# Expert rows in half blocks: eight blocks shared by two experts

## The chip, the cores and the metric

The kernel runs on one core of one Trainium2 chip. Times are device microseconds of the whole program. A time given for a kernel is the median of several runs; a profile is one execution, and its span runs from the first to the last instruction. PE multiplies matrices (PEld loads its weights), DVE, ACT and POOL are the vector, scalar and GpSimd engines, and SP issues most transfers. POOL also issues every transfer whose rows are chosen by an index (a gather or a scatter).

## The reference

Two layers act on `x`, 8 x 256 x 512 in single precision. The first is a gated long convolution; only what comes after it is touched by the change. The second is a mixture of experts on 2,048 tokens of 512 numbers:

```python
scores = sigmoid(xf @ gate_w.T)                    # 2048 x 8
topk_w, topk_idx = top_k(scores, 2)
topk_w = topk_w / (topk_w.sum(-1, keepdims=True) + 1e-20) * 2.5
shared_out = silu(xf @ shared_wg.T) * (xf @ shared_wu.T) @ shared_wd.T
h = silu(einsum('td,efd->etf', xf, exp_wg)) * einsum('td,efd->etf', xf, exp_wu)
all_out = einsum('etf,edf->etd', h, exp_wd)        # 8 experts, width 352
out = x + shared_out + sum of topk_w * all_out of the token's two experts
```

`xf` is the layer-normalised result of the first layer. Every token goes to two of the eight experts, so 4,096 rows in all are to be multiplied, and how many fall to each expert is known only when the scores are.

## The kernel before

**Stages.** The convolution runs over 32 heads with PE as its work horse (`conv_products`, L393). While it runs, 16 tiles of 128 tokens are normalised, written to `xn_d` in DRAM, and routed in four chunks. The shared expert's products (`up_step` L678, `down_step` L725) are a list of steps spread over the later heads; the last ones come after the convolution. Then come the experts' blocks.

**The table.** `route_places` (L647) gives every pair of token and expert a place: expert e owns 2,048 places, filled in order. POOL scatters an entry (token number, weight) of eight bytes to each place of a DRAM `table`. After the last chunk, `block_experts` (L778) works out from the eight counts, on DVE, which expert each block of 128 rows has (`ek`) and which column of the table it takes (`pick`, one column per block with a single one in it). `load_table` (L823) brings the table back as `tab`, 128 rows of 128 places. `quarters_of` (L839) spreads its token numbers by quarters of 32 rows, and `slots` (L850) multiplies them with `pick`: the results are, for each block, the DRAM rows to gather (`src`), the rows of the output to add to (`row`) and the weights (`gate`).

**The blocks.** There are at most 39 blocks: `NBLK` at L37. The first 36 (`NSURE`) always run; the last three are in a branch (`rest_of_blocks`, L1201), which every engine reaches ahead of block 18 and takes only if the count says so. A block has, in order:

- `gather` (L1048): four indirect transfers of POOL, each 128 rows of 128 numbers.
- `load_ek` (L1062): PE reads the expert into a register.
- `block_T` (L1069): DVE transposes the rows by 32 x 32 squares into `xT`.
- `block_up` (L1110): eight products of PE, 128 rows by 352 columns, whose weights' address is the register's; ACT's sigmoid and two multiplications on DVE.
- `block_hT` (L1153): sixteen small transposes on DVE.
- `block_down` (L1168): three products of PE, 128 rows by 512 columns; ACT scales the result by `gate`; POOL scatters the 128 rows into `out`, adding to what is there.

The trace shows a single-precision product as two records. What order the work has is written out by hand in the last loop (L1212): in round k, rows are gathered for block k + 4 and transposed for block k + 2, block k is multiplied up, and block k - 2 down. Each engine runs its instructions in the order written. Buffers: four for the gathered rows, three for `xT`, `h`, `hT` and `y`, and two banks pairs for PE's results. All scatters write the same tensor `out`, at rows that the program text doesn't know.

**Around the change.** The last steps of the shared expert stand between the table and the first block: three steps, then `slots`, one step, the first gathers, and four down steps with `block_T` of the first three blocks between them (L1036 to L1090). Constants come from POOL at the start (`iota`, L176).

Of the kernel before, what the change touches and what calls it, by code (L numbers as in the profile page):

```python
# [36 lines left out]
NBLK = 2 * NTOK // P + NEXP - 1  # L37
CPE = NTOK // P

NSURE = NBLK - 3  # L40
Q = 32
NQ = P // Q

# [22 lines left out]
def tile_xattn_moe(  # L66
# [123 lines left out]
    blockno = iota("blockno", NBLK, 1, 0)  # L190
    thresh = iota("thresh", CPE, P, 0)
    quarter = const.tile([P, 1], F32, name="quarter")
    for q in range(NQ):
        G.memset(quarter[q * Q : (q + 1) * Q], float(q))
# [582 lines left out]

    def block_experts():  # L778
        def g(name, s, dtype=F32):
            return const.tile(s, dtype, name=name)  # L780

        V.tensor_tensor(place, place, base, ALU.subtract)
        full = g("full", [P, NEXP, CPE])
# [9 lines left out]
        ends = g("ends", [P, NEXP])  # L793
        V.tensor_copy(ends[:, 0:1], nblk[:, 0:1])
        for e in range(1, NEXP):
            V.tensor_tensor(ends[:, e : e + 1], ends[:, e - 1 : e], nblk[:, e : e + 1], ALU.add)
        gap = g("gap", [P, NEXP])
        V.tensor_scalar(gap, nblk, -1.0, float(CPE), ALU.mult, ALU.add)
        full_k = [P, NBLK, NEXP - 1]
        past = g("past", full_k)  # L800
# [3 lines left out]
            ends[:, : NEXP - 1].unsqueeze(1).to_broadcast(full_k),  # L804
            ALU.is_ge,
        )
        ek = g("ek", [P, NBLK], I32)
        with nc.allow_low_precision(reason="whole numbers below 8"):
            V.tensor_reduce(ek, past, AX.X, ALU.add)
        V.tensor_tensor(  # L810
            past, past, gap[:, : NEXP - 1].unsqueeze(1).to_broadcast(full_k), ALU.mult
        )
        col = g("col", [P, NBLK])
        V.tensor_reduce(col, past, AX.X, ALU.add)
        V.tensor_tensor(col, col, blockno, ALU.add)
        pick = g("pick", [P, NBLK])
        V.tensor_scalar(pick, col, lane, None, ALU.is_equal)

        used = g("used", [P, 1], I32)
        V.tensor_copy(used, ends[:, NEXP - 1 :])  # L820
        return ek, pick, used

    def load_table():  # L823

        tab = const.tile([P, P, 2], F32, name="tab")
        ins = S.dma_start(
            out=tab.rearrange("p b f -> p (b f)"),
            in_=table.rearrange("(p b) f -> p (b f)", b=P),
        )
        for s in scatters:  # L830
            tc.add_manual_dep(
                ins.ins,
                s.ins.name,
                mybir.DependencyInfo(mybir.DependencyClass.Sync, mybir.DependencyReason.DATA),
                reason="the table's rows come from all of them",
            )
        return tab

    def quarters_of(tab):  # L839
        by_quarter = const.tile([P, NQ, NQ, Q], F32, name="by_quarter")  # L840
        V.tensor_copy(
            by_quarter,
            tab[:, :, 0]
            .rearrange("p (c b) -> p c b", b=Q)
            .unsqueeze(2)
            .to_broadcast([P, NQ, NQ, Q]),
        )
        return by_quarter

    def slots(tab, by_quarter, pick):  # L850
        def g(name, s, dtype=F32):
            return const.tile(s, dtype, name=name)


        ps = ps_tp.tile([P, 2 + NQ, NBLK], F32, tag="tp", name="slots_ps")
        for f in range(2):
            T.matmul(ps[:, f, :], lhsT=tab[:, :, f], rhs=pick, start=True, stop=True)
        for c in range(NQ):
            T.matmul(
                ps[:, 2 + c, :],  # L860
                lhsT=by_quarter[:, c].rearrange("p q b -> p (q b)"),
                rhs=pick,
                start=True,
                stop=True,
            )

        spare = g("spare", [P, NBLK])
        V.tensor_scalar(spare, ps[:, 0, :], 0.0, lane, ALU.is_equal, ALU.mult)
        row = g("row", [P, NBLK], I32)
        V.scalar_tensor_tensor(row, ps[:, 0, :], float(NTOK), spare, ALU.add, ALU.add)  # L870
        gate = g("gate", [P, NBLK])
        V.tensor_copy(gate, ps[:, 1, :])
        src = g("src", [P, NQ, NBLK], I32)
        for c in range(NQ):
            V.tensor_scalar_add(spare, ps[:, 2 + c, :], float(NTOK))
            V.tensor_scalar(src[:, c], spare, float(NQ), quarter, ALU.mult, ALU.add)
        return src, row, gate
# [24 lines left out]
    skip_products(0)  # L902

# [129 lines left out]
    ek, pick, used = block_experts()  # L1033
    tab = load_table()
    settle()
    for n in range(3):  # L1036
        step()
        if n == 2:
            by_quarter = quarters_of(tab)
        settle()  # L1040
    src, row, gate = slots(tab, by_quarter, pick)
# [6 lines left out]
    def gather(k):  # L1048
        if k >= NBLK:
            return  # L1050
        xgs[k] = (rows if k < NSURE else spare).tile([P, NQ, P], F32, tag="xg", name=f"xg_{k}")
        for c in range(NQ):
            G.indirect_dma_start(  # L1053
                out=xgs[k][:, c, :],
                out_offset=None,
                in_=xn_q,
                in_offset=bass.IndirectOffsetOnAxis(ap=src[:, c, k : k + 1], axis=0),
# [4 lines left out]
    def load_ek(k):  # L1062
        if k < NBLK:
            eks[k] = nc.values_load(
                ek[0:1, k : k + 1], engines=[PE], min_val=0, max_val=min(k, NEXP - 1),
                skip_runtime_bounds_check_because="a block's expert is a count of at most seven",
            )

    def block_T(k):  # L1069

        if k >= NBLK:
            return
        own = (rows, 3) if k < NSURE else (spare, 1)
        xTs[k] = own[0].tile([P, NLB, NQ, Q], F32, tag="xT", name=f"xT_{k}", bufs=own[1])
        V.transpose(
            xTs[k].rearrange("p k c b -> p c k b"),
            xgs.pop(k).rearrange("p c (k a) -> p c k a", a=Q),
# [3 lines left out]
    AHEAD = 2  # L1081
    for k in range(AHEAD + 2):
        gather(k)
    for k in range(AHEAD):
        load_ek(k)
    for k in range(TPC):
        step()
        settle()
        if k <= AHEAD:
            block_T(k)  # L1090
# [19 lines left out]
    def block_up(k, last):  # L1110
        n = min(k + 1, NEXP)
        ps = (ps_b if k < NSURE else ps_spare).tile([P, 2, L], F32, tag="up", name=f"up_{k}")
        wk = wgu_sb[:, :n].rearrange("p e f -> p (e f)")
        for m in range(2):
            for j in range(NLB):
                T.matmul(  # L1116
                    ps[:, m, :FF],
                    lhsT=xTs[k][:, j].rearrange("p c b -> p (c b)"),
                    rhs=wk[:, bass.ds(eks[k] * NGU + (m * NLB + j) * FF, FF)],
                    start=(j == 0),  # L1120
                    stop=(j == NLB - 1),
                )
        hk = (blk if k < NSURE else spare).tile([P, FF], F32, tag="h", name=f"h_{k}")
        A.activation(hk, ps[:, 0, :FF], AF.Sigmoid)  # L1124
        V.tensor_tensor(hk, hk, ps[:, 0, :FF], ALU.mult)  # L1125
        xTs.pop(k)
        if not last:
            V.tensor_tensor(hk, hk, ps[:, 1, :FF], ALU.mult)
# [24 lines left out]
    def block_hT(k):  # L1153
# [3 lines left out]
        for c in range(NQ):  # L1157
# [10 lines left out]
    def block_down(k):  # L1168
        n = min(k + 1, NEXP)
# [4 lines left out]
        wk = wd_sb[:, :n].rearrange("p e f -> p (e f)")  # L1174
        hT = hTb.pop(k)
        for ft, (_, fw) in enumerate(F_TILES):
            T.matmul(  # L1177
                ps,
                lhsT=hT[:fw, ft].rearrange("p c b -> p (c b)"),
                rhs=wk[:fw, bass.ds(eks[k] * NWD + ft * L, L)],  # L1180
                start=(ft == 0),
                stop=(ft == NF - 1),
            )
        y = (blk if k < NSURE else spare).tile([P, L], F32, tag="y", name=f"ys_{k}")
        A.activation(y, ps, AF.Copy, scale=gate[:, k : k + 1])
        G.indirect_dma_start(  # L1186
# [132 lines left out]
```

## Time and profile before

| what | value |
|---|---|
| median of 3 runs | 807.13 us (806.12 to 812.91) |
| profiled execution, own time | 791.86 us |
| its span | 790.1 us |
| PE busy | 768.2 us, 97% |
| DVE, POOL, ACT busy | 535.1, 472.7, 201.8 us |
| experts' up products (L1116) | 176.2 us, 576 records |
| experts' down products (L1177) | 98.6 us, 216 records |
| gathers (L1053) | 144, 1,019 ns each |
| scatters (L1186) | 36, 1,616 ns each |
| first up product, last record of a down product | 511.13, 776.5 us |

A line of the page's groups has the source line, the engine and the operation, what is written and read by the program's names, how many there were, then their busy time, the mean length of one in ns, and the idle time of the engine ahead of them with what ended it. Mean lengths on PE are longer than the distance from one record to the next, since products overlap. A line of a timeline has the start, the length, the engine, the line, the operation and, in brackets, the idle time before. The 68 halves and 36 blocks that the text counts come from the reference's own inputs.

### The profile page before, as it was taken

To read this page: it belongs to the slowest core of one execution; us is meant where nothing else is said; L and a number is where in the kernel's file an instruction comes from. 1 tells how busy PE (TensorE), PEld (TensorE's weight loads), DVE (VectorE), ACT (ScalarE), POOL (GpSimd) and SP (SyncE) were. 2 spreads that over 40 slices of the span, in tenths; PEclk is the share of its full clock that TensorE was granted. 3 is DMA by queue.
4 is the path that set the end of the run, shared out by engine and by line. 5 is a ranking of instruction groups with operands and counts; after the bars stand their busy time and mean duration, and the time that the engine had idled before them with its cause. 6 is when DMAs were issued, how large, how long until landed. Compare 5 with 4: busy or idle time off the path is not lost. (4 is left out here: it accounts for less than half of the span.)

```text
span 790.1 us, 8491 instructions
## 1 busy us (share of the span) xinstructions
PE 768.2 (97%) x2383; PEld 353.7 (45%) x2383; DVE 535.1 (68%) x1209; ACT 201.8 (26%) x382; POOL 472.7 (60%) x474
## 2 busy tenths in 40 slices
PE   8999999999999999999999999999999999999993
PEld 4333334433333443333443444365555555555551
DVE  3678868768567768557765163189778778778760
ACT  2222353443153344134323200011111111111111
POOL 7877784378373469372640043756777757777721
PEclk9999999999999999999999999999999999999997
DMA  7585433324414234312100780396444434344433
GB/s 253 174 298 175 153 114 127 120 35 127 147 46 140 92 50 140 114 47 87 63 12 27 304 347 24 103 263 135 73 68 77 74 56 74 69 75 78 69 45 40
DMA packets 52143, 89.10 MB, mean 113 GB/s; under 512 B 8833, under 2 KB 24065, under 8 KB 50945
## 3 DMA queue, kind: packets, MB, share of 16 engines
q1 hardware_dynamic: 36960, 61.77, 24.4%
q0 software_dynamic: 10816, 18.92, 13.9%
q10 hardware_dynamic: 4320, 7.87, 2.9%
q8 instruction: 21, 0.34, 0.2%
q14 instruction: 26, 0.20, 0.1%
HBM read 66.34 MB, written 22.18 MB: 112 GB/s over the span
## 5 line engine op out<-in xcount | busy, mean ns | idle before, releaser
L416 PE MATMUL cv<-kv,tz 128*64 128x512 f32 (+2 forms) x720 | 190.1, 607 | 0.2 <-POOL kv L376 0.2
L1053 POOL DMA_INDIRECT xg<-xn_d,src x144 | 146.8, 1019 | 62.2 <-issue 46.4
L1116 PE MATMUL up<-wgu_sb,xT 128*128 (+1 forms) x576 | 176.2, 459 | 2.3 <-DVE x L757 1.4
L688 PE MATMUL gu<-xfT,wsh 128*128 128x512 f32 x352 | 156.7, 598 | 1.2 <-issue 1.2
L1160 DVE STREAM_TRANSPOSE hTb<-h 32x96 f32<-32x96 f32 (+1 forms) x560 | 146.3, 261 | 8.2
L376 POOL TENSOR_TENSOR kv<-vT,ctxT 128x512 f32<-128x512 f32 x128 | 133.1, 1072 | 19.0 <-issue 6.2
L1116 PEld LDWEIGHTS up<-wgu_sb,xT 128*128 128x128 f32 x576 | 109.0, 190 | 73.3 <-issue 17.1
L416 PEld LDWEIGHTS cv<-kv,tz 128*64 128x64 f32 (+2 forms) x720 | 60.8, 150 | 119.5 <-issue 97.7
L688 PEld LDWEIGHTS gu<-xfT,wsh 128*128 128x128 f32 x352 | 67.1, 192 | 85.7 <-issue 84.5
L1177 PE MATMUL y<-wd_sb,hTb 128*128 (+3 forms) x216 | 98.6, 592 | 0.8 <-ACT hTb L1149 0.8
L478 DVE TENSOR_TENSOR prod<-cv,ctxT 128x1024 f32<-128x1024 f32 x64 | 78.2, 1221 | 16.4 <-PE cv L416 14.7
L662 POOL DMA_INDIRECT table<-entries,to x32 | 31.8, 993 | 90.5 <-DVE at L658 81.9
L1186 POOL DMA_INDIRECT out_dram<-ys,row x36 | 58.2, 1616 | 41.6 <-issue 24.0
L487 DVE TENSOR_REDUCE convT<-prod 128x128 f32<-128x1024 f32 x64 | 78.1, 1220 | 2.2
L732 PE MATMUL dn<-wshd,hT 128*128 128x512 f32 x160 | 70.2, 593 | 0.0
L1177 PEld LDWEIGHTS y<-wd_sb,hTb 128*128 128x128 f32 (+1 forms) x216 | 41.0, 190 | 43.1 <-issue 34.7
L1124 ACT ACTIVATE h<-up 128x352 f32<-128x352 f32 x36 | 16.7, 463 | 167.0 <-PE up L1116 167.0
L702 ACT ACTIVATE sg<-gu 128x512 f32<-128x512 f32 (+1 forms) x24 | 14.3, 596 | 166.4 <-PE gu L688 166.4
L532 POOL TENSOR_TENSOR skip<-ctxT,w 128x512 f32<-128x512 f32 x16 | 17.2, 1076 | 59.4 <-ACT w L524 30.2
L1125 DVE TENSOR_TENSOR h<-h,up 128x352 f32<-128x352 f32 x36 | 18.6, 517 | 43.6 <-ACT h L1124 43.6
L416 PE MATMUL cv<-kv,td 128*128 128x512 f32 x88 | 47.2, 618 | 0.0
L732 PEld LDWEIGHTS dn<-wshd,hT 128*128 128x128 f32 x160 | 30.2, 190 | 37.6 <-issue 37.6
(149 smaller groups left out, 602.3 us busy)
## 6 DMA issues: line engine op xcount, KB each, us to landing
tz<-in_toep_dram SPq DMA_DIRECT2D x32, 384.0 KB, 3.4
wgu_sb<-in_egu_dram SPq DMA_DIRECT2D x8, 1408.0 KB, 16.3
ctxT<-in_cT_dram SPq DMA_DIRECT2D x16, 384.0 KB, 4.8
x<-in_xv_dram SPq DMA_DIRECT2D x16, 256.0 KB, 3.6
x<-in_x_dram SPq DMA_DIRECT2D x16, 256.0 KB, 4.7
xn_d<-xn ACTq DMA_DIRECT2D x16, 256.0 KB, 2.3
out_dram<-x SPq DMA_DIRECT2D x16, 256.0 KB, 2.4
wd_sb<-in_ed_dram SPq DMA_DIRECT2D x8, 512.0 KB, 11.8
```

The costliest lines, as they stand in the source:

```text
L376: G.tensor_tensor(kv[:, mb], vT[t][:, at, :, cols].unsqueeze(2).to_broadcast([P, B, NH, NH]), ctxT[t][:, at, :, cols].unsqueeze(3).to_broa ...
L416: T.matmul(banks[lb][cols], lhsT=w, rhs=x, start=first, stop=left[lb][here[0]] == 0,)
L478: V.tensor_tensor(prod, ps.rearrange("p k b j i -> p (k b) j i"), ctxT[t][:, 2 + 2 * n : 4 + 2 * n, :, cols] .rearrange("p k b i -> p (k b ...
L487: V.tensor_reduce(convT[t][:, two, :, cols].rearrange("p k b j -> p (k b) j"), prod, AX.X, ALU.add)
L662: ins = G.indirect_dma_start(out=table, out_offset=bass.IndirectOffsetOnAxis(ap=to[:, i : i + 1], axis=0), in_=entry[:, i, n, :], in_offse ...
L688: T.matmul(ps, lhsT=wsh[:, k, m0 : m0 + m], rhs=rhs[k], start=(k == 0), stop=(k == NLB - 1))
L732: T.matmul(ps, lhsT=hTs[c][:, ft, i * P : (i + 1) * P], rhs=wshd[:, ft, :], start=(ft == 0), stop=False,)
L1053: G.indirect_dma_start(out=xgs[k][:, c, :], out_offset=None, in_=xn_q, in_offset=bass.IndirectOffsetOnAxis(ap=src[:, c, k : k + 1], axis=0 ...
L1116: T.matmul(ps[:, m, :FF], lhsT=xTs[k][:, j].rearrange("p c b -> p (c b)"), rhs=wk[:, bass.ds(eks[k] * NGU + (m * NLB + j) * FF, FF)], star ...
L1160: V.transpose(hT[q * Q : (q + 1) * Q, :n, c], hk[c * Q : (c + 1) * Q, q * NF * Q : (q * NF + n) * Q].rearrange("p (t a) -> p t a", a=Q),)
L1177: T.matmul(ps, lhsT=hT[:fw, ft].rearrange("p c b -> p (c b)"), rhs=wk[:fw, bass.ds(eks[k] * NWD + ft * L, L)], start=(ft == 0), stop=(ft = ...
L1186: G.indirect_dma_start(out=out, out_offset=bass.IndirectOffsetOnAxis(ap=row[:, k : k + 1], axis=0), in_=y, in_offset=None, bounds_check=NT ...
```

## The change

Rows are counted in halves of 64. Every expert's first half goes to a fixed place: the second half of one of eight shared blocks (`NMIX`), whose expert there is a constant of the program. What is left of an expert fills whole blocks of its own, of which 26 (`NPURE`) always run; whole blocks beyond the 26 and odd halves are put one after another into the first halves of the eight shared blocks, with their expert in a register, and, when these are full, into 16 half blocks in the branch. So 34 blocks always run in place of 36. The eight shared blocks stand at positions 7, 10, 13 and so on to 28 of the order.

A shared block multiplies each of its two halves with its own expert's weights, by products of 64 columns of the array each, and its result goes out by two scatters of 64 rows, the second of which is issued in the middle of the next round's gathers. The table is read back shifted by 64 places, by three transfers. The arithmetic on the counts has a second part (`half_experts`), and the shared blocks' rows a second set of products (`half_slots`).

The core of the diff:

```diff
+HALVES = 2 * NTOK // P
+NPURE, NMIX, NCOND = 26, NEXP, 16
+NSURE, NHALF = NPURE + NMIX, NMIX + NCOND
+NBLK = NPURE + NHALF
...
-    blockno = iota("blockno", NBLK, 1, 0)
-    thresh = iota("thresh", CPE, P, 0)
-    quarter = const.tile([P, 1], F32, name="quarter")
-    for q in range(NQ):
-        G.memset(quarter[q * Q : (q + 1) * Q], float(q))
...
+    def half_experts(nblk, ends):
+        odd = g("odd", [P, NEXP])
+        V.scalar_tensor_tensor(odd, nblk, -float(P), place, ALU.mult, ALU.add)
+        V.tensor_scalar(odd, odd, float(HP), None, ALU.is_gt)
...
+        for e in range(NEXP):
+            at = NEXP + e
+            V.tensor_tensor(
+                ends[:, at : at + 1],
+                ends[:, at - 1 : at] if e else begin,
+                odd[:, e : e + 1],
+                ALU.add,
+            )
...
+        any_half = g("any_half", [P, 2, NHALF])
+        for n in range(2):
+            V.tensor_scalar(any_half[:, n], half, float(-n), lane2, ALU.add, ALU.is_equal)
+        first_half = g("first_half", [P, NEXP])
+        V.tensor_scalar(first_half, first_block, lane, None, ALU.is_equal)
...
+        return eh, any_half, first_half, used
...
         tab = const.tile([P, P, 2], F32, name="tab")
+        body = (P - 1) * P
+        for to, first, n in (
+            (tab[: P - 1], HP, body),
+            (tab[P - 1 :, :HP], HP + body, HP),
+            (tab[P - 1 :, HP:], 0, HP),
+        ):
+            ins = S.dma_start(
+                out=to.rearrange("p b f -> p (b f)"),
+                in_=table[first : first + n].rearrange("(p b) f -> p (b f)", b=to.shape[1]),
+            )
...
+    def half_slots(any_half, first_half):
+        ps = ps_tp.tile([P, 2, NQ, NHALF], F32, tag="tp", name="halves_ps")
+        for f in range(2):
+            quarter = [by_quarter[f][:, c].rearrange("p q b -> p (q b)") for c in range(NQ)]
+            for c in range(2):
+                for n in range(2):
+                    T.matmul(
+                        ps[:, f, c],
+                        lhsT=quarter[2 * n + c],
+                        rhs=any_half[:, n],
+                        start=(n == 0),
+                        stop=(n == 1),
+                    )
+                T.matmul(
+                    ps[:, f, 2 + c, :NMIX],
+                    lhsT=quarter[2 + c],
+                    rhs=first_half,
+                    start=True,
+                    stop=True,
+                )
+        rows_h = g("rows_h", [P, NHALF])
+        for n, m in enumerate((NHALF, NMIX)):
...
+            for c in range(2):
+                A.copy(rows_h[c * Q : (c + 1) * Q, :m], ps[c * Q : (c + 1) * Q, 0, 2 * n + c, :m])
+                at = slice((2 * n + c) * Q, (2 * n + c + 1) * Q)
+                A.copy(gate[at, cols], ps[at, 1, 2 * n + c, :m])
...
+            lay_rows(row[at, to], rows_h[at, :m], f"spare_{n}", at)
...
     skip_products(0)
+    lane2 = iota("lane2", 1, 0, 2)
+    blockno = iota("blockno", NPURE, 1, 0)
+    halfno = iota("halfno", NHALF, 1, 0, base=2 * NPURE)
+    thresh = iota("thresh", CPE, P, 0, base=P)
+    expert_thresh = iota("expert_thresh", NEXP - 1, HALVES, 0, base=HALVES)
+    first_block = iota("first_block", NEXP, CPE, 0, base=-1)
...
+    def gather(b):
+        xgs[b] = (rows if b < NSURE else spare).tile([P, NQ, P], F32, tag="xg", name=f"xg_{b}")
+        for c in range(rows_in(b) // Q):
+            if c == 3:
+                send_late()
             G.indirect_dma_start(
...
+    FIRST = 7
+    seq = list(range(NPURE))
+    for i in range(NMIX):
+        seq.insert(FIRST + 3 * i, NPURE + i)
...
+        if k == 0:
+            eh, any_half, first_half, used = half_experts(nblk, ends)
+            turn_quarters(1, tab, A.copy)
+        if k == 2:
+            half_slots(any_half, first_half)
...
             for j in range(NLB):
+                for at, e in eks[k]:
+                    T.matmul(
+                        ps[at, m, :FF],
+                        lhsT=xTs[k][:, j].rearrange("p c b -> p (c b)")[:, at],
+                        rhs=weights(wgu_sb, k, e, (m * NLB + j) * FF, FF),
+                        start=(j == 0),
+                        stop=(j == NLB - 1),
+                    )
...
+        def send(at, col):
+            G.indirect_dma_start(
+                out=out,
...
+                in_=y[at],
...
+        send(eks[k][0][0], k)
+        if len(eks[k]) > 1:
+            late.append((send, slice(HP, P), k + NHALF))
...
-        with tc.If(more > NSURE):
-            for k in range(NSURE, NBLK):
+        with tc.If(more > 2 * NPURE + NMIX):
+            for b in range(NSURE, NBLK):
...
-        if k == NSURE // 2:
+        if k == NSURE - 8:
             rest_of_blocks()
```

The down products are written for the two halves in the same way.

## The prediction

> **What bounds the kernel now.** I read the page's busy shares first, then the stages by windows, then the timelines of PE and POOL in the last third, and the DMA view around one load. Two lines of the page (busy time, share, instructions; then a group with its count, busy time and mean) and one row of the windows (busy us of PE, PEld, DVE, ACT, POOL, then clock and DMA share):
>
> ```profile
> PE 768.2 (97%) x2383; PEld 353.7 (45%) x2383; DVE 535.1 (68%) x1209; ACT 201.8 (26%) x382; POOL 472.7 (60%) x474
> ...
> L1186 POOL DMA_INDIRECT out_dram<-ys,row x36 | 58.2, 1616 | 41.6 <-issue 24.0
> ```
> ```profile
> 542.00:630.00 88.00, 88.00 (x266) 50.15 (x265) 71.80 (x231) 13.80 (x24) 69.39 (x62) 1.00 0.43 74
> ```
>
> PE is never idle in the expert stage: it binds there. But POOL's 69 of 88 us hide something. In the next timelines (start, length, engine, line, operation, idle before), PE's down products of two blocks in a row start 7.31 us apart, and POOL's scatters 7.25 us (7.241 over 28 of them, less the branch), with only 0.3 us of handover between its instructions:
>
> ```profile
> 591.24 2.74 PE L1177 MATMUL y<-wd_sb,hTb 128*128 x6
> ...
> 598.55 1.88 PE L1177 MATMUL y<-wd_sb,hTb 128*128 x4
> ```
> ```profile
> 560.78 1.63 POOL L1186 DMA_INDIRECT out_dram<-ys,row  x1 [0.30 <-issue]
> 562.72 1.06 POOL L1053 DMA_INDIRECT xg<-xn_d,src  x1 [0.30 <-issue]
> 564.09 1.01 POOL L1053 DMA_INDIRECT xg<-xn_d,src  x1 [0.31 <-issue]
> 565.40 1.01 POOL L1053 DMA_INDIRECT xg<-xn_d,src  x1 [0.30 <-issue]
> 566.71 1.01 POOL L1053 DMA_INDIRECT xg<-xn_d,src  x1 [0.30 <-issue]
> 568.03 1.63 POOL L1186 DMA_INDIRECT out_dram<-ys,row  x1 [0.30 <-issue]
> ```
>
> So POOL, with four gathers (1.313 us each with handover) and a scatter (1.94 us) a block, has 0.07 us a block to spare. Nor can scatters go closer. At the end, with the gathers gone:
>
> ```profile
> 769.27 1.55 POOL L1186 DMA_INDIRECT out_dram<-ys,row  x1 [3.94 <-issue]
> 774.71 1.55 POOL L1186 DMA_INDIRECT out_dram<-ys,row  x1 [3.88 <-ACT hTb L1149]
> 780.14 1.55 POOL L1186 DMA_INDIRECT out_dram<-ys,row  x1 [3.89 <-issue]
> ```
>
> They follow each other every 5.44 us: 1.55 us of issue, then 3.89 us until the transfer has landed (4.7 us from its start by the tile's view) and the next may start. All write `out` at rows known only at run time, so each waits for the last. With 780.14 the end of the kernel hangs on this chain, not on PE, done at 776.5.
>
> Ahead of the experts, PE stands at the table's load:
>
> ```profile
> 483.52 0.64 PE L857 MATMUL slots_ps<-pick,tab 128*128 128x39 f32 x4 [1.10 <-DMA tab<-table]
> 483.99 1.06 PE L859 MATMUL slots_ps<-pick,by_quarter 128*128 128x39 f32 x8
> 484.88 5.38 PE L688 MATMUL gu<-xfT,wsh 128*128 128x512 f32 x8
> ```
>
> **What the skill says.** *DMA: Bandwidth & Descriptors*, "Why a DMA increments its semaphore by 16 and not by 1": a transfer issued by SP runs on the largest number of engines up to 16 that divides its slowest dimension, so 128 partitions take 16 and 127 take one. The DMA view of 481 to 484 us agrees for 128:
>
> ```profile
> DMA  0000000000000000013323687740000000000000
> ...
> q1 hardware_dynamic: 144, 0.13, 12.6%
> ```
>
> The load's 128 rows and 16 small packets take 12.6% of 16 engines times 3 us, 6.05 us in all, some 46 ns a row, within 11 slices of 0.075 us; no run shows 127. The price of a row alone, 42 to 43 ns for 1 KiB, is in *Advanced Engine Details and Errata*, "Clock Domains". *TensorEngine Tiling*, "Key Properties": half-width tiles run independently, changing the tiling mode drains the array. The trace agrees:
>
> ```profile
> 96.99 1.02 PE L416 MATMUL cv<-kv,td 128*128 128x512 f32 x2
> 97.94 2.96 PE L416 MATMUL cv<-kv,tz 128*64 128x512 f32 x16
> 100.83 1.12 PE L416 MATMUL cv<-kv,td 128*128 128x512 f32 x2
> ```
>
> The 16 records (eight 128x64, eight 64x64) start to next start take 2.89 us where the same work at full use (0.429 us a full record, as in the down products: 8/2 + 8/4 of them) takes 2.57. By the groups split by form, 128x64 records cost 244 ns of busy time against 461 for full ones: they run in pairs. *Perfetto Trace Analysis*, "DMA Instruction — SWDGE (GPSIMD)": the recorded time of such a transfer is the writing of its descriptors, not the movement. So 1.62 us of a scatter should fall with its rows.
>
> **The change, part by part.** Routing the reference's inputs gives 554, 506, 572, 453, 532, 450, 523 and 506 rows per expert: 36 blocks of 128, or 68 halves of 64. Eight are fixed; 28 whole blocks and 4 odd halves leave exactly 60, so the branch (over 60) isn't taken, as before (36 of 36).
>
> *Two blocks fewer.* PE loses 2 x 7.31 = 14.6 us; POOL's steps are counted below.
>
> *Eight shared blocks on PE.* Each of their 22 half-width products pairs with its neighbour, so a block costs one block. Mode changes: about 0.15 us in and 0.19 out in the stretch above; both an up and a down stretch, 0.68 us a block, 5.4 us in all. Bounds: 0, and 58 us if nothing pairs; PE gains 9.2 us net. Register arithmetic stays at one instruction for each register-addressed product, hidden in the queue today (PE waits 0.9 us on it in all).
>
> *POOL's chain.* A shared block keeps four gathers and has two scatters of 64 rows, the second put between the third and fourth gather of the next round. Each waits for the landing before it. Not in this trace: a scatter of 64 rows. Its issue lies between 0.81 (half) and 1.62 us; I take 0.9, near half. The wait behind it lies between 2.3 (landing halved) and 3.89; I take 3.1. First to second: 0.9 + 0.31 + 3 x 1.313 = 5.15 us (the landing is covered). Second to the next block's: 0.9 + 3.1 = 4.0, since one gather covers only 2.5. Together 9.15, 1.91 more than 7.24. Behind that wait stand the next gathers. From block 1's scatter to block 29's, before, took 207.8 us, with 5.13 for the branch; to the last, 33.2 more: 241.1. After: 26 steps of 7.24 (188.2), 7 x 1.91 (13.4), the branch 5.1, then, gathers gone, 5.44 + 4.0 + 4.0 + 4 x 5.44 = 35.2: **241.9**. PE over the same rounds, 26 x 7.31 + 7 x 0.68 + 0.9 at the branch, is 196: POOL comes 11 us behind, under the two rounds that gathers run ahead, so PE isn't starved, but the end is POOL's: +0.8 us instead of -9.2. The bounds give -7 and +20.
>
> *The table's load* becomes three: 127 rows on one engine, 127 x 42 ns = 5.3 us and two short ones behind, instead of 0.8: **+4.6 us**, all of it PE's idle time, since `slots` stands next in its queue and DVE's copy waits too. Bound below: +0.7 us, two more issues of 0.33, if it is spread.
>
> *half_slots* adds 12 products, 24 records at 0.113 us ((484.88 - 483.52)/12): **+2.7 us** on PE, between down steps that have no gap.
>
> *Clock.* At 484.88 eight records took 5.2 us against 3.5: the half clock after the idle stretch cost 1.7 us. *A longer idle time* costs between nothing and as much again; +0.5.
>
> *At nothing:* half_experts, some 29 DVE instructions of 0.2 to 0.5 us, 7 us, in DVE's idle 493.8 to 500; if it ran over, the x additions slip, with 3 us to spare before half_slots. Its ACT copies lie in ACT's idle 25 us; `lay_rows` ends before the down step (5.5 us) does. The iotas moved past skip_products (about 1.2 us of POOL) fit its 4.39 us wait for vT. `slots` on DVE is 1 us shorter, before gathers that POOL does well ahead. The branch, larger inside, is skipped as before; it moves from block 18 to round 26, past eight rounds of each queue, and costs POOL the same wait for its last landing (640.45 to 647.52 between two of its transfers) and PE 0.9 us; both are counted above.
>
> Sum: 0.8 + 4.6 + 2.7 + 0.5 = +8.6 us on 791.86 (span 790.1 and 1.7 around it), 800.5. The runs' median, 807.13, lies 15.3 us over the profiled run, unexplained; I carry that over unchanged: **815.7 us**.
>
> **Rivals.** (B) *PE keeps the end*, not slower: if a shared block's POOL round stays under 22.61 - 14.48 = 8.13 us (three PE rounds less two of POOL's), say with issue 0.6 and wait 2.0, or if halves don't wait for each other, PE's -9.2 stands: -9.2 + 7.8 = -1.4, 805.7; with a spread load 801.8. For: equal bytes, and descriptors counted by rows. Against: 5.44 between whole scatters is mostly waiting. (C) *A half costs POOL as much as a whole*: 11.4 us a shared round, gathers late, PE starved: +20 + 7.8, 835. For: fixed parts of issue and landing. Against: the skill's account. (D) *The load is spread after all*: 8.6 - 3.9, 811.8. That products don't pair: +49 on PE, near 862; the convolution speaks against it, 1 in 50, within C.
>
> **Chances.** Forecast 0.62, B 0.16, C 0.12, D 0.10. Measurement tells about 1% (8.1 us) from no change. Within the forecast (issue 0.8 to 1.1, clock) 0.44 lies above 1%, 0.18 below; C is slower; D 0.02 of it; B same but for 0.04 with a spread load. Faster 0.04, same 0.38, slower 0.58. The range 804 to 829 takes in B, D and the forecast's dearer halves (+20), and leaves C out.
>
> **What would show it.** A tab landing near 7 us, PE idle near 5.7 before slots_ps; scatters near 0.9 us, a POOL wait of 1.5 us ahead of the scatter after each late one; shared up products of 4.9 to 5.1 us; last scatter some 11 us after PE. A tab landing of 2 us, or scatters close behind PE's last product, prove me wrong.

## The result and the profile after

The changed kernel takes **831.21 us** (829.92 to 833.45, 6 runs) where the kernel before takes 806.62 us (804.50 to 813.59, 6 runs): ratio **1.0285**, 95% interval 1.0237 to 1.0334. The prediction was 815.7 us with a range of 804 to 829. The direction was right, the size was not, and the time lies outside the range.

One thing has to be known to read the numbers below. In some sets of runs, each on one chip, PE stands still for about 15 us just ahead of the experts' first block (a halt, in what follows), and in others it doesn't; the profile of before had no halt, the profile of after has it. A kernel's time is therefore read as a ratio to the kernel before on the same chip, and the change in time is accounted for with the pair of traces in which neither kernel halts (spans of 789.6 and 811.0 us; in those runs the ratio is 1.0277, interval 1.0258 to 1.0297).

The page of the changed kernel, its busy shares and the group of the scatters:

```profile
PE 770.9 (93%) x2539; PEld 343.2 (41%) x2539; DVE 526.2 (64%) x1199; ACT 200.8 (24%) x387; POOL 473.6 (57%) x477
...
L1336 POOL DMA_INDIRECT out_dram<-ys,row x42 | 65.5, 1560 | 75.2 <-DMA wd_sb<-in_ed_dram 27.0
```

POOL has two blocks fewer and is still as busy as before: 42 scatters in place of 36, each 1,560 ns in place of 1,616. Half the rows did not make half the issue. The mixed mean hides it; the timeline of POOL around one shared block (start, length, engine, line, operation, idle before) shows it:

```profile
609.71 1.50 POOL L1336 DMA_INDIRECT out_dram<-ys,row  x1 [0.30 <-issue]
611.52 1.05 POOL L1181 DMA_INDIRECT xg<-xn_d,src  x1 [0.30 <-issue]
612.87 1.01 POOL L1181 DMA_INDIRECT xg<-xn_d,src  x1 [0.30 <-issue]
614.19 1.01 POOL L1181 DMA_INDIRECT xg<-xn_d,src  x1 [0.30 <-issue]
615.50 1.50 POOL L1336 DMA_INDIRECT out_dram<-ys,row  x1 [0.30 <-issue]
617.31 1.04 POOL L1181 DMA_INDIRECT xg<-xn_d,src  x1 [0.30 <-issue]
620.08 1.59 POOL L1336 DMA_INDIRECT out_dram<-ys,row  x1 [1.73 <-ACT ys L1332]
```

The two scatters of 64 rows take 1.50 us each (a whole one takes 1.63). From the first to the second it is 5.79 us, from the second to the next block's 4.58: 10.37 us in place of 7.24. What the last of them waited for can't be read from this line: ACT stood still for 10.15 us here, in the trace with the halt, and had scaled that block's rows only by 619.80. In the trace without a halt (e10 below) ACT had scaled the same block's rows by 598.79, and the step is the same 4.58 us:

```profile
598.73 1.50 POOL L1336 DMA_INDIRECT out_dram<-ys,row  x1 [0.30 <-issue]
...
603.31 1.59 POOL L1336 DMA_INDIRECT out_dram<-ys,row  x1 [1.74 <-ACT h L1271]
```

So this scatter waits for the landing of the one before, whatever the line names as its releaser; e4 below shows it by taking that wait away.

PE, over 88 us of the experts' stage, is still without a gap in its records (columns as for the kernel before: PE, PEld, DVE, ACT, POOL, clock, DMA share, GB/s), and a shared block costs it hardly more than a pure one:

```profile
577.80:665.80 88.00, 88.00 (x345) 45.05 (x344) 65.55 (x213) 13.04 (x23) 65.61 (x58) 1.00 0.37 65
```
```profile
604.56 2.80 PE L1323 MATMUL y<-wd_sb,hTb 128*64 x12
607.19 4.90 PE L1263 MATMUL up<-wgu_sb,xT 128*64 x32
612.02 2.85 PE L1323 MATMUL y<-wd_sb,hTb 128*128 x6
...
626.85 2.80 PE L1323 MATMUL y<-wd_sb,hTb 128*64 x12
```

Half-width products do run in pairs: the up products of a shared block take 4.90 us, like those of a pure one. From one shared block's down products to the next one's, three blocks on, it is 22.29 us, where three pure blocks take 3 x 7.31 = 21.93: 0.4 us for a shared block. The first two lines show a likely reason: with a shared block at every third position, its down products stand right ahead of the next shared block's up products, so PE changes its mode once in and once out a shared block, not twice.

So a shared block takes POOL about 3 us more than a pure one, POOL falls behind, and in the last four blocks PE runs out of rows. Timelines of PE, of DVE's transposes, and of POOL's last scatters:

```profile
781.93 2.82 PE L1323 MATMUL y<-wd_sb,hTb 128*128 x6 [3.36 <-DVE hTb L1307]
```
```profile
758.53 0.71 DVE L1213 STREAM_TRANSPOSE xT<-xg 128x512 f32<-128x512 f32 x1 [8.41 <-DMA xg<-xn_d,src]
...
775.70 0.71 DVE L1213 STREAM_TRANSPOSE xT<-xg 128x512 f32<-128x512 f32 x1 [3.85 <-DMA xg<-xn_d,src]
```
```profile
787.94 1.45 POOL L1336 DMA_INDIRECT out_dram<-ys,row  x1 [4.47 <-ACT ys L1332]
791.88 1.43 POOL L1336 DMA_INDIRECT out_dram<-ys,row  x1 [2.50 <-DMA out_dram<-ys,row]
796.25 1.56 POOL L1336 DMA_INDIRECT out_dram<-ys,row  x1 [2.94 <-DMA out_dram<-ys,row]
...
818.39 1.56 POOL L1336 DMA_INDIRECT out_dram<-ys,row  x1 [3.82 <-issue]
```

DVE waits for gathered rows, PE for DVE, and the last scatter starts 13.3 us after PE's last product has ended (805.06). Before, it started 3.1 us after (780.14 and 777.09; the 776.5 of the prediction is where that last record starts).

Ahead of the experts, PE stands at the table's load. Timeline of SP's queue and of PE; then the DMA view from 481 to 491 us; then a row of the windows:

```profile
481.17 2.42 SPq L890 DMA_DIRECT2D tab<-table  x3
```
```profile
489.38 1.02 PE L934 MATMUL slots_ps<-pick,tab 128*128 128x26 f32 x4 [7.30 <-DMA tab<-table]
490.23 1.89 PE L936 MATMUL slots_ps<-pick,rows_by_quarter 128*128 128x26 f32 x8
491.93 6.08 PE L687 MATMUL gu<-xfT,wsh 128*128 128x512 f32 x8
```
```profile
GB/s 0 0 0 0 8 0 12 4 25 25 16 12 25 25 25 25 20 25 25 25 25 25 25 25 25 25 20 25 25 12 0 0 0 0 0 0 0 0 0 0
...
q1 hardware_dynamic: 132, 0.13, 3.8%
```
```profile
490.00:495.00 5.00, 5.00 (x14) 3.42 (x15) 1.68 (x6) 0.00 (x0) 1.95 (x2) 0.50 0.05 13
```

The 132 packets run at a nearly steady 25 GB/s from about 483 to 488.3 us, 41 ns for 1,024 bytes: one DMA engine, as foreseen (3.8% of 16 engines times 10 us is 6.1 us of packets, 46 ns each). PE idles 7.30 us in place of 1.10, and then runs at half clock: the eight `gu` records behind the slots take 6 us in place of 3.5 at full clock.

**The account**, from the two traces without a halt (before, then after, in us from the span's start):

| stretch | before | after | difference | predicted |
|---|---|---|---|---|
| to the first slots product (the load) | 484.86 | 489.64 | +4.8 | +4.6 |
| from there to the first down step (clock) | 4.87 | 8.42 | +3.5 | +0.5 |
| from there to the first up product (half_slots) | 21.04 | 23.71 | +2.7 | +2.7 |
| from there to the last scatter (POOL's chain) | 268.77 | 279.40 | +10.6 | +0.8 |
| last scatter to the end | 10.06 | 9.83 | -0.2 | 0 |
| span | 789.6 | 811.0 | **+21.4** | +8.6 |

The fourth row can be worked out: two blocks fewer give POOL 2 x 7.24 = 14.5 us, eight shared blocks at 10.28 us (the mean of seven in that trace; the eighth, behind the last gathers, takes 8.45 where a pure one takes 5.5) cost 8 x 3.04 = 24.3, and the round with the branch costs 0.9 more (13.10 and 12.20 us): +10.7.

### The profile page after: what moved, and what is told of

Same layout as the page of the kernel before. It is cut to its first block, busy times and chain, and to the rows that moved or that the text cites. A ratio compares the mean times of both kernels' runs of the same rounds, so it can differ in the third digit from the quotient of the medians.

```text
span 828.4 us, 8780 instructions
## 1 busy us (share of the span) xinstructions
PE 770.9 (93%) x2539; PEld 343.2 (41%) x2539; DVE 526.2 (64%) x1199; ACT 200.8 (24%) x387; POOL 473.6 (57%) x477
## 5 line engine op out<-in xcount | busy, mean ns | idle before, releaser
L1263 PE MATMUL up<-wgu_sb,xT 128*128 (+3 forms) x672 | 172.1, 469 | 13.9 <-DVE x L756 9.7
L1181 POOL DMA_INDIRECT xg<-xn_d,src x136 | 139.4, 1025 | 67.4 <-issue 38.4
L1307 DVE STREAM_TRANSPOSE hTb<-h 32x96 f32<-32x96 f32 (+1 forms) x528 | 138.0, 261 | 7.8
L1263 PEld LDWEIGHTS up<-wgu_sb,xT 128*128 128x128 f32 (+1 forms) x672 | 99.7, 174 | 91.7 <-issue 41.7
L1336 POOL DMA_INDIRECT out_dram<-ys,row x42 | 65.5, 1560 | 75.2 <-DMA wd_sb<-in_ed_dram 27.0
L1323 PE MATMUL y<-wd_sb,hTb 128*128 (+5 forms) x252 | 94.7, 600 | 5.6 <-DVE hTb L1307 3.4
L1323 PEld LDWEIGHTS y<-wd_sb,hTb 128*128 128x128 f32 (+3 forms) x252 | 35.0, 170 | 52.7 <-issue 47.0
L1332 ACT ACTIVATE ys<-y,gate 128x512 f32<-128x512 f32 x34 | 23.4, 688 | 83.1 <-DMA out_dram<-ys,row 38.9
```

The lines of the kernel that those rows point to most:

```text
L1181: G.indirect_dma_start(out=xgs[b][:, c, :], out_offset=None, in_=xn_q, in_offset=bass.IndirectOffsetOnAxis(ap=src[:, c, b : b + 1], axis=0 ...
L1263: T.matmul(ps[at, m, :FF], lhsT=xTs[k][:, j].rearrange("p c b -> p (c b)")[:, at], rhs=weights(wgu_sb, k, e, (m * NLB + j) * FF, FF), star ...
L1307: V.transpose(hT[q * Q : (q + 1) * Q, :n, c], hk[c * Q : (c + 1) * Q, q * NF * Q : (q * NF + n) * Q].rearrange("p (t a) -> p t a", a=Q),)
L1323: T.matmul(ps[at], lhsT=hT[:fw, ft].rearrange("p c b -> p (c b)")[:, at], rhs=weights(wd_sb, k, e, ft * L, L)[:fw], start=(ft == 0), stop= ...
L1336: G.indirect_dma_start(out=out, out_offset=bass.IndirectOffsetOnAxis(ap=row[: at.stop - at.start, col : col + 1], axis=0), in_=y[at], in_o ...
```

## The experiments

Four of them repeat a kernel unchanged, to place the 15 us between the profile of before and its median.

**e0_before_again**, the kernel before:

> The kernel before, unchanged. In its first profile the execution took 791.86 us where its other runs have a median of 807. Theory 1: about 15 us lie between a profiled execution and the others in every case; then the span is again 790 us within 2. Rival: the first profile was a lucky one; then this span is near 805.

Measured: 794.93 us with a span of 793.2, and the runs beside it on this chip had a median of 792.99 (15 runs). A profiled execution is no faster than others. The 15 us came with the first set of runs.

**e1_after_again**, the changed kernel on the same chip:

> The changed kernel, unchanged. In its first profile PE stands still for about 14 us behind half_slots (last down step to first expert product, 514.6 to 536.2 us), and its span is 828.4, 38 us over the span before, where the medians are 24.6 us apart. Theory 1: the pause belongs to that one execution; then the first expert product starts near 522 and the span is about 814. Rival: the pause belongs to the kernel (a wait that half_slots brings); then it starts near 536 again and the span is near 828.

Measured: 816.27 us, span 814.6, first up product at 523.70, and no halt of PE. From the down step behind half_slots to the first up product it is 6.98 us here (516.72 to 523.70) and 21.61 in the profile of after (514.58 to 536.19). These 14.6 us are therefore no part of the change. The halves are the same: 1.49 us of issue, 5.76 and 4.47 us to the next (750.56, 756.32, 760.79).

**e2_spread_load**: the table's 127 rows as 112 and 15.

```diff
-        body = (P - 1) * P
+        body, most = (P - 1) * P, 7 * P // 8
         for to, first, n in (
-            (tab[: P - 1], HP, body),
+            (tab[:most], HP, most * P),
+            (tab[most : P - 1], HP + most * P, body - most * P),
```

> The changed kernel with the table's 127 rows loaded as 112 and 15, so that they divide by 16 and by 15. Theory 1: the load on one DMA engine costs 5 us and the longer half clock behind it 1 to 2; PE's wait ahead of slots falls from 7.3 us to about 2.5 and the time by 5 to 7 us, to about 825. Rival: the load's time is the landing of three transfers in a row, not the rows on one engine; then PE's wait stays above 6 us and the time at 831.

Measured: 809.12 us (806.09 to 810.49), ratio 1.0222, interval 1.0185 to 1.0259: 7.2 us less than the one run of the changed kernel on this chip (816.27; the 825 of the expectation started from 831). PE's idle time at the slots fell to 2.65 us, although SP now issues four loads (1.43 us). In the profiled executions the first up product comes 8.5 us earlier than in e1 (515.18 and 523.70) and the span is 10.2 us shorter (804.4 and 814.6); beside the changed kernel's trace on another chip (521.77, 811.0) both differences are 6.6. Single executions differ by a few us, so this shows that what the load delays at the start arrives at the end, where POOL sets it, but not to the last us.

**e3_one_scatter**: a shared block's two halves of row numbers are laid into one column of 128, and the block is scattered in one piece.

```diff
-                A.copy(rows_h[c * Q : (c + 1) * Q, :m], ps[c * Q : (c + 1) * Q, 0, 2 * n + c, :m])
                 at = slice((2 * n + c) * Q, (2 * n + c + 1) * Q)
+                A.copy(rows_h[at, :m], ps[at, 0, 2 * n + c, :m])
...
-            at = slice(0, HP)
-            to = slice(NPURE + n * NHALF, NPURE + n * NHALF + m)
-            lay_rows(row[at, to], rows_h[at, :m], f"spare_{n}", at)
+            at = slice(n * HP, (n + 1) * HP)
+            lay_rows(row[at, cols], rows_h[at, :m], f"spare_{n}", at)
...
-        send(eks[k][0][0], k)
-        if len(eks[k]) > 1:
-            late.append((send, slice(HP, P), k + NHALF))
+        send(slice(0, n), k)
```

> The changed kernel with one scatter of 128 rows for a shared block in place of two of 64 (the row numbers of the second half are laid on partitions 64 to 127; no token stands twice in a block with these inputs). Theory 1: POOL's chain sets the end, 10.4 us a shared block where 7.24 is a whole one's; the time falls by about 8 x 3.1 us less what PE then takes over, to 806 to 810, and the last scatter follows PE's last product as closely as before. Rival: PE's mode changes and half_slots cost the time; then it stays above 825.

Measured: **790.97 us** (790.15 to 792.80, 12 runs), ratio 0.9981, interval 0.9964 to 0.9998. On a chip where the changed kernel takes 816 (one run), this gives back 25 us, as theory 1 had it: its 806 to 810 started from 831, and from 816 they are 791 to 795. The last scatter starts 2.6 us after PE's last product has ended (780.46 and 777.87). A token of one half can also stand in the other half of the same block, in principle; with these inputs none does, and a kernel for other inputs would have to make sure of it. POOL's timeline around a shared block is that of a pure one again:

```profile
586.54 1.62 POOL L1335 DMA_INDIRECT out_dram<-ys,row  x1 [0.30 <-issue]
...
593.77 1.63 POOL L1335 DMA_INDIRECT out_dram<-ys,row  x1 [0.30 <-issue]
...
601.00 1.63 POOL L1335 DMA_INDIRECT out_dram<-ys,row  x1 [0.30 <-issue]
```

So eight extra scatters, nothing else of the change, cost 25 us here, and 22 in the account above against e8 below (279.40 and 257.04 us from the first up product to the last scatter).

**e4_late_aside** takes the wait away and leaves the issue: the second half goes to another tensor.

```diff
+    aside = dram.tile([P, L], F32, name="aside")
+    S.dma_start(out=aside, in_=zero)
+    lane_i = iota("lane_i", 1, 0, 1, dtype=I32)
...
+            first = at.start == 0
...
-                out=out,
+                out=out if first else aside,
...
```

> The changed kernel, but the second scatter of a shared block goes to a scratch tensor in DRAM, so that neither it nor the next scatter waits for the other's landing; its issue on POOL stays. (The first 64 rows of every expert are therefore left out of the result.) Theory 1, issue and wait both count: a shared block's two scatters then take from one to the next block's 7.24 us (four gathers 5.25, two issues of 1.49 with 0.3 of handover each, 3.6: 8.85 us) in place of 10.36, so eight blocks give back 8 x 1.5 = 12 us and the time lies near 804 (the changed kernel 816, with one scatter a block 791). Rival, the waits alone set it: the issue is absorbed, and the time comes down to 791 to 794. Second rival, the issue alone: no change, 814 to 818.

Measured: 821.02 us (820.15 to 822.83), ratio 1.0144, interval 1.0085 to 1.0202, on a chip where the kernel before takes 808.76. The changed kernel is at 1.0285 there (its first runs, on a chip of the same pace), so 1.4% or 11.4 us come back, with some 5 to 18 us left open by the two intervals together; 12 were expected from issue and wait together, 25 from the wait alone, none from the issue alone. The total is weaker evidence than it looks: this trace has halts (PE stands for 7.19 us at the branch, where the profile of after has 0.85, and five scatters wait 1.7 to 2.3 us for ACT), POOL catches up in them, and the last scatter follows PE's last product by 2.5 us. The split is better read from the rounds. Where POOL is behind, the round is the worked-out one:

```profile
657.07 1.48 POOL L1340 DMA_INDIRECT out_dram<-ys,row  x1 [0.30 <-issue]
662.83 1.47 POOL L1340 DMA_INDIRECT aside<-ys,lane_i  x1 [0.30 <-issue]
665.95 1.59 POOL L1340 DMA_INDIRECT out_dram<-ys,row  x1 [0.30 <-issue]
```

8.88 us in place of 10.3: of the 3.0 us that a shared block costs POOL over a pure one's 7.24, the landing behind the second half is 1.4, the issue of a second scatter the other 1.6.

**e5_before_127**: the kernel before, its one load issued as 127 rows and one.

```diff
-        ins = S.dma_start(
-            out=tab.rearrange("p b f -> p (b f)"),
-            in_=table.rearrange("(p b) f -> p (b f)", b=P),
-        )
+        rows_of = table.rearrange("(p b) f -> p (b f)", b=P)
+        for at in (slice(0, P - 1), slice(P - 1, P)):
+            ins = S.dma_start(out=tab[at].rearrange("p b f -> p (b f)"), in_=rows_of[at])
...
```

> The kernel before, but its one load of the table's 128 rows is issued as 127 rows and then one. Theory 1: 127 rows keep to one DMA engine; PE's idle time ahead of the slots' products rises from 1.6 to between 7 and 8 us, half-speed products behind it last longer, and the time rises by 6 to 8 us, to 799 to 801 (ratio 1.008 to 1.010). Rival: what the changed kernel loses there comes from its three issues by SP (2.4 us) and not from the number of rows: the idle time is near 2.5 us and the time within 2 us of before.

Measured: 820.50 us (819.69 to 821.48), ratio 1.0141, interval 1.0083 to 1.0200: 11.7 us, with 6.7 to 16.2 in the interval, which the expected 6 to 8 just meets. It was a chip on which PE halts: the trace has the halt, PE idle for 5.46 us ahead of the slots' products, and four waits of 2.0 to 2.1 us ahead of a scatter that e9's trace doesn't have. The rival, within 2 us of before, is out.

**e9_before_127_again**, the same kernel on a chip on which it doesn't:

> The kernel before with the load of the table as 127 rows and one, once more. Where PE makes no halt of 15 us ahead of the experts, theory: idle time ahead of the slots' products 7 to 8 us, half speed for 10 us or more behind it, time 6 to 9 us over before (ratio 1.008 to 1.011). Rival: 11.7 us as in the first runs (1.014), because a longer idle time also brings on the later halt.

Measured: 800.43 us (798.99 to 801.24), ratio 1.0101, interval 1.0080 to 1.0122: **7.9 us**, as expected. Beside the trace of before on this chip the slots' products start 4.4 us later (489.30 and 484.86), and from there to the first down step it is 8.79 us in place of 4.87: 3.9 more, at half clock. Timeline of PE, and the windows behind it:

```profile
489.30 1.05 PE L856 MATMUL slots_ps<-pick,tab 128*128 128x39 f32 x4 [7.08 <-DMA tab<-table]
```
```profile
490.00:495.00 5.00, 5.00 (x14) 3.34 (x14) 3.21 (x13) 0.00 (x0) 1.32 (x2) 0.50 0.00 0
```

A load of 127 rows and one in place of 128, in a kernel that is otherwise the one before, costs 1%. That it is the rows and not the second issue is shown by e2, whose four loads leave PE idle for 2.65 us.

**e6_both**: e2 and e3 together (their two diffs).

> The changed kernel with both of its costs removed: the table's rows loaded as 112, 15 and two halves, and one scatter of 128 rows a block, shared or not. If the two costs lie one after the other (theory): the one-scatter kernel's 791 less the 7 us that the spread load gave, 784, ratio 0.989 to the kernel before. Rival: POOL, and not PE, sets the end of the experts' stage, and its chain starts with the gathers, which the earlier table moves as well, so the same 784; but if PE's start isn't what sets POOL's chain, 788 to 791.

Measured: 806.80 us (803.98 to 810.63, 22 runs), ratio 0.9980, interval 0.9961 to 0.9999. A miss of both: 784 and 788 to 791 beside 793 are ratios of 0.989 and 0.994 to 0.998, and the theory's is outside the interval; the rival's upper end fits, but not for its reason. The trace shows PE halted ahead of the experts (first up product at 530.14) and five later waits of about 2 us ahead of a scatter that this kernel doesn't have in e8.

**e8_both_again**, the same kernel on a chip without these halts:

> The changed kernel with the table's rows loaded as 112, 15 and two halves, and one scatter of 128 rows a block, once more beside the kernel before and the changed kernel on one chip. In its first runs PE stood still for 15 us ahead of the experts' first block, and for some 2 us at six later places, where no row of the trace has a cause. Theory: those halts belong to the chip that the runs fell on and not to the kernel; without them the kernel takes 783 to 786 where the one before takes 793 (ratio 0.988 to 0.991). Rival: they come with this kernel's order of work, and the ratio stays near 0.998.

Measured: **782.77 us** (781.32 to 785.67), ratio **0.9882**, interval 0.9862 to 0.9902. The theory held. Of the page, and of the timelines of PE and POOL:

```profile
PE 759.0 (97%) x2539; PEld 338.4 (43%) x2539; DVE 527.8 (68%) x1199; ACT 201.1 (26%) x387; POOL 462.8 (59%) x469
```
```profile
485.33 0.62 PE L935 MATMUL slots_ps<-pick,tab 128*128 128x26 f32 x4 [2.60 <-DMA tab<-table]
```
```profile
765.51 1.56 POOL L1336 DMA_INDIRECT out_dram<-ys,row  x1 [4.45 <-ACT hTb L1296]
770.96 1.55 POOL L1336 DMA_INDIRECT out_dram<-ys,row  x1 [3.89 <-issue]
```

PE is at 97% again, and its last product ends at 768.39, 2.6 us ahead of the last scatter: the end follows PE, as in the kernel before. From the first up product (513.92) to the last scatter it is 257.04 us, 11.7 less than before; PE's own account gives 2 x 7.31 less 8 x 0.4, 11.4. Half blocks do pay, once their two costs are taken out, but only in the runs without halts, where this kernel is the fastest of all; in those with halts the same kernel gained nothing (e6, 0.998). So halts don't weigh on every kernel alike.

**e7_late_32**: 32 rows in the second scatter.

```diff
-            late.append((send, slice(HP, P), k + NHALF))
+            late.append((send, slice(HP, HP + Q), k + NHALF))
```

> The changed kernel with only 32 of the 64 rows in the second scatter of each shared block (the other 32 rows are left out of the result). Theory 1, the issue of a scatter is nearly all fixed: 1.62 us at 128 rows, 1.49 at 64, so 1.40 to 1.45 at 32, and the distance from it to the next scatter stays near 4.5; time 812 to 816. Rival, the issue is counted by rows with a start of its own below 64: 0.75 to 1.1 us at 32 rows, and a time near 808.

Measured: 827.60 us (one run) beside 808.76 for the kernel before, a ratio of 1.0233. POOL's timeline:

```profile
659.71 1.50 POOL L1336 DMA_INDIRECT out_dram<-ys,row  x1 [0.30 <-issue]
...
665.49 1.41 POOL L1336 DMA_INDIRECT out_dram<-ys,row  x1 [0.30 <-issue]
...
669.41 1.60 POOL L1336 DMA_INDIRECT out_dram<-ys,row  x1 [1.15 <-issue]
```

The issue takes 1.63 us for 128 rows, 1.50 for 64, 1.41 for 32: nearly all of it is fixed, as theory 1 had it. What does shrink with the rows is the landing: the distance to the next scatter is 3.92 us (3.8 to 3.9 in six of seven such rounds, 4.6 in the first), where 64 rows have 4.5. Theory 1 had that wrong, and the absolute times of both theories were meant for the other chip. Where in the round the second scatter stands was not varied.

**e10_after_third** and **e11_before_third**, both kernels beside e8 and e9, unchanged:

> The changed kernel itself, for a ratio on the chip of the two runs ahead of it. Theory: the ratio to before is 1.028 to 1.030 with or without PE's halt of 15 us, since both kernels have it on a chip that shows it (816 beside 793, 831 beside 807). Rival: the halt belongs to the changed kernel's own profile, and the ratio falls to 1.01 on a chip without it.

> The kernel before, for its trace beside these. Theory: where its time is near 807 the trace shows PE halted for 15 us between the shared expert's last products and the first block's (first up product at 526 to 530 in place of 511 to 514), and where it is near 793 it shows no halt. Rival: the 15 us lie elsewhere, spread over the experts' blocks.

Measured: 813.90 us (812.69 to 814.98), ratio 1.0277, interval 1.0258 to 1.0297, as the theory had it: for this kernel the ratio is the same with the halt and without. The kernel before took 791.28 and showed no halt, which agrees with the theory but tests only its second half; a trace of the kernel before with a halt was not had.

## Why the prediction was wrong

By its own steps, with the measured value beside each:

- *"It lies between 0.81 (half) and 1.62 us; I take 0.9, near half."* **This step failed.** It is 1.49. The page of the Trainium skill from which the prediction took it (*Perfetto Trace Analysis*, "DMA Instruction — SWDGE (GPSIMD)") says that the recorded time is the writing of descriptors; the prediction went on from there to "should fall with its rows", which was its own inference. The runs contradict it: 13% less for a quarter of the rows (1.41 us in e7, 1.63 for a whole one). Two scatters times 0.59 us is 1.2 us a shared block. The bounds were right and the point within them wrong. Rival C ("a half costs POOL as much as a whole"), at 0.12, came nearer in time with its 835, in part by luck: its shared round of 11.4 us is as far from the measured 10.28 as the forecast's 9.15, and what it had too much there was in part made up by the clock's 3 us, which it lacked as well.
- *The wait behind a half, 3.1 us.* Right: 3.0 to 3.1 (4.58 less 1.50 in one round, 4.48 less 1.49 in another); e4 shows what it is worth.
- *A shared round of 9.15 us.* 10.28. Over the seven that lie between block 1's scatter and the end of the gathers that is 7.9 us more than the prediction's sum. The branch (5.9 in place of 5.1) and the tail (36.5 in place of 35.2) add 0.8 and 1.3. From block 1's scatter to the last one the prediction had 241.9 us; the trace without a halt has 251.6 (549.54 to 801.17).
- *"PE isn't starved."* Wrong in the same way: at 10.3 us a shared round POOL's lag outgrows the rounds that gathers run ahead, and PE waits in the last four blocks. It moved PE's last product and added little to the end, which was POOL's already: the one scatter behind it that waited for PE's rows came after a step of 5.99 us (764.70 to 770.69), where the first step behind the gathers takes 5.6 and 5.8 in the two traces of the kernel before.
- *The load, +4.6 us.* Right in mechanism and size: +4.8, one engine, 46 ns a packet over all and 41 in the steady stretch (42 taken). The Trainium skill's statement on 127 partitions (*DMA: Bandwidth & Descriptors*, "Why a DMA increments its semaphore by 16 and not by 1") is borne out by e2, e5 and e9.
- *The clock, +0.5.* Mis-sized: +3.5. Behind the longer idle time (e10) the clock is 0.67, 0.50 and 0.81 in the three stretches of 5 us from 485 on, which is 10.2 us at half speed, and the shared expert's step runs in it. The prediction bounded the term by 1.7 more, from a profile of the kernel before that had some half clock there already (from its slots to its first down step 6.57 us; against that, the profile of after has 8.47, +1.9). The trace of the kernel before in the account has a clock of 1.00 from 485 on, so there was more to lose. Short idle times don't settle it: behind 2.65 us (e2) the clock from 485 to 490 was 0.72, behind 2.60 us (e8) it was 1.00.
- *half_slots, +2.7 us.* 2.67. *At nothing:* half_experts lies in DVE's idle time as written (500.93 to 507.24 in the profile of after), and the x addition behind it waits for PE.
- *Mode changes, 0.68 us a shared block.* 0.4: the price of a change was about right, but the prediction counted two stretches a shared block where the order leaves one; off the path that sets the end.
- *The 15.3 us carried over unchanged.* Right to carry: the changed kernel has the halt on such a chip (the profile of after), and so has the kernel before with the split load (e5); for the kernel before as it stands only the times, 807 and 809, say so.

A slip without weight: with its own terms the prediction's 862, for products that don't pair, would be 864 (807.1 + 49 + 7.8).

The terms make up the miss: 9.8 of POOL's chain and 3.2 of load and clock are 13.0, against 801.1 (792.5 + 8.6) and 813.9 measured on the chip without halts, 12.8 apart. On the first chip the miss was 15.5; the 2.7 left over lie in how the halt meets the rest, and were not settled.

Rival B ("PE keeps the end") named the right condition. It is the state that e8 reaches, by dropping the second scatter.

## What to carry to other kernels

Count a scatter as one issue of nearly fixed length (here from 32 to 128 rows), and add its landing if the next one writes the same tensor: split in two, 128 rows took 2 x 1.49 us of issue in place of 1.63, and a second landing to wait for. On an engine with 0.07 us a round to spare that decides everything. Where a duration isn't in the trace and scaling it by size would make the change pay, work out the answer for no scaling first. Check how many rows a load has before it is cut: with 112 and 15 rows in place of 127 the kernel took 7 to 8 us less.

## What was not expected of the hardware

- **The issue of a scatter hardly depends on its rows**: 1.63, 1.50 and 1.41 us for 128, 64 and 32 rows of 2 KB. Landing does: scatters to one tensor, back to back at the end, follow each other after 5.4 to 5.7 us at 128 rows (1.56 of issue, 3.8 to 4.1 of wait); behind 64 rows it is 4.0 for the first half of a block (1.45 and 2.5) and 4.4 for the second (1.43 and 3.0).
- **A halt of PE of some 15 us that comes with the set of runs.** The same kernel, before with the split load, has its last x addition on DVE at these times on a chip that took 820.5 us and on one that took 800.4 (timelines of DVE, the halted one first):

```profile
531.99 1.29 DVE L757 TENSOR_TENSOR x<-dn,x 128x512 f32<-128x512 f32 x2 [21.79 <-remote]
```
```profile
517.78 1.29 DVE L757 TENSOR_TENSOR x<-dn,x 128x512 f32<-128x512 f32 x2 [6.50 <-PE dn L745]
```

  DVE waits there for PE's last products of the shared expert. But these come no later in the halted trace: their records end at 516.56 there and at 517.74 in the other, and DVE goes on 15.4 us and 0.04 us after that. In the other four traces with a halt (after, e4, e6, e7) DVE stands for 20 to 22 us ahead of what it reads of half_slots, and many of PE's records of the last down steps lie 1.4 to 2.1 us apart in place of 0.43. POOL's gathers go on without a break meanwhile, and in all five DVE goes on 2.9 to 3.4 us after the last gather of that unbroken line ends. Whether the gathers have to do with it was not tried, and the cause stays open.
